# A two-layer bottleneck on one core: the first loads and the attention inputs change queues

## The chip, the core and the metric

The kernel runs on one core of a Trainium2 chip. A core has five engines with instruction streams of their own: TensorE (PE) for matrix products, VectorE (DVE) and ScalarE (ACT) for elementwise work, GpSimd (POOL) and SyncE (SP). They share an on-chip memory of 128 partitions (SBUF), the accumulators that PE writes (PSUM), and sixteen DMA engines that move data between SBUF and the main memory. A DMA is issued by an instruction in the stream of SP, ACT or POOL, and an instruction waits its turn in its stream: nothing behind a waiting instruction of an engine can start.

The metric is the device time of one execution in microseconds (us). The kernel before takes 2476.17 us, the median of 9 runs that lie between 2469.25 and 2484.35.

## The reference, cut to what matters

Sixteen images of 1024 channels and 32x32 pixels go through two bottleneck layers, all in float32. The first has a self-attention over a 3x3 neighbourhood in its middle, the second a 3x3 convolution.

```python
# layer 0
h = relu(bn(conv1x1(x, w_conv1)))                    # 1024 -> 256 channels
q, k = relu(bn(conv1x1(h, wq))), relu(bn(conv1x1(h, wk)))
v = bn(conv1x1(h, wv))
attn = softmax(sum over the 8 channels of a head of q * (unfold3x3(k) + pos_h + pos_w))
h = relu(bn(sum over the 9 places of unfold3x3(v) * attn))
x = relu(bn(conv1x1(h, w_conv3)) + x)                # 256 -> 1024
# layer 1
out = relu(bn(conv1x1(x, w1)))                       # 1024 -> 256
out = relu(bn(conv3x3(out, w2)))
x = relu(bn(conv1x1(out, w3)) + x)                   # 256 -> 1024
```

## The kernel before, in words

An image's 1024 channels are eight chunks of 128 channels (one per partition) by 1024 pixels, 512 KB each. The work of an image falls into stages on PE, and one list (`stages`) fixes their order for all sixteen images:

- conv1 (C): the eight chunks `x` times the weights `w1`, summed in PSUM (`reduce_part`, L346). ACT turns the sum into `h` (L975).
- qk (Q): from `h` the keys (`bnk`), the queries (`q`) and the position terms (`pos`); v (V): the values (`bnv`). The products are at L432 and L470.
- fused (F): the attended tensor `a` times `w3` plus the residual `s` (L377), and at once the first sum of layer 1 (L346).
- wino (W): the 3x3 convolution of four images together in Winograd form, `V` times `U` (L723).
- u3 (U): the last product plus the residual `r` (L377).

The stages run C, Q, V for images 0 to 3, then F of finished images between the C, Q, V of later ones. "C8 Q8 W0 V8" is a stretch of the list: image 8's queries are made directly before the Winograd stage of images 0 to 3, which is directly before image 8's values. Images 11 and 14 stand so before the stages of images 4 to 7 and 8 to 11.

The attention itself is DVE's work and runs beside PE's stages. It needs its inputs in another layout: one row per group of heads and quarter of the image. So `q`, `bnk`, `bnv` and `pos` are written to main memory and read back ("relay"). The writes: SP issues `bnk` and `bnv` (L456) and `q` (L490, two DMAs per image), ACT issues `pos` (L484, two per image). All reads back are issued by POOL (`relay`, L520). The position terms take a step that matters here: ACT writes them over the first half of `q` (`by_offset`, L479), so this instruction waits until the first `q` DMA has read that half.

POOL issues nearly all bulk transfers: the later images' chunks, the residuals and the Winograd forms (L322), and the results (L397). At a time eight tiles are there for loaded chunks (`credits`); a load is issued when the tile is free.

What happens before the first product is written by hand in `at_first`. ACT issues the first image's chunks, and between them the loads of the nine taps of the 3x3 weights (`load_taps`, two times three DMAs of 384 KB, L248), and then the last weights of both layers (`load_scaled`, four of 512 KB, L211). SP issues the first weights `w1` in eight pieces of 128 KB, one per chunk (L126), then `wqk` and `wv` (L128). `scale_rows` then turns a scale of 1024 channels, which lies over partitions, into one row in main memory (L221, `row`, 1024 elements of 4 bytes), and reads that row back into all partitions (L223, `scales`), once for each layer. From the taps ACT and DVE make the Winograd weights (`winograd_weights`, L259 to L269, in turns), which go to main memory (L281, `uw`, twelve DMAs of 768 KB); DVE then scales the last weights (L231).

In the built program each DMA of SP and ACT has one of eight semaphores, given out in turn over both engines, and each DMA of POOL one of eight others. A DMA waits until the one that had its semaphore before has landed. So a DMA of ACT can wait for one of SP.

Of the kernel before, what the change touches and what calls it, by code (L numbers as in the profile page):

```python
# [13 lines left out]
P = 128  # L14
# [4 lines left out]
NW = WID // P  # L19
# [6 lines left out]
CHUNKS = 8  # L26
NJ = 4
# [4 lines left out]
NPOS = 4  # L32
G = P // HEAD_DIM
# [38 lines left out]
def sa_bottleneck_kernel(ctx: ExitStack, tc: tile.TileContext, x, w1t, wqkvt, w3t, u1t, u2t, u3t, params, out):  # L72
    nc = tc.nc
# [25 lines left out]
    def source(name, half):  # L99

        if name[0] == "U":
            return uw[int(name[1]), half]
        if name in ("w3", "u3"):
            return ws[name == "u3", half]
        if name[1] == "1":
            src = {"w1": w1t, "u1": u1t}[name].rearrange("(c p) n -> p c n", p=P)
            return src[:, half * NC // 2 : (half + 1) * NC // 2]
        at = {"wqk": slice(0, 2 * WID), "wv": slice(2 * WID, 3 * WID)}[name]
        return wqkvt.rearrange("(c p) n -> p c n", p=P)[:, :, at]

    def more_weights():

        if not queue:
            return
        key = name, of, half = queue.pop(0)
        t = wpool.tile([P, HW], F32, tag="w", name=f"{name}{half}_{of[0]}")
        src = source(name, half)
        n, k = src.shape[-1], 1
        for d in src.shape[1:-1]:
            k *= d  # L120
        view = t[:, : k * n].rearrange("p (c n) -> p c n", n=n)
        if len(src.shape) == 4:
            view = t.rearrange("p (m j o) -> p m j o", m=NW, j=2)
        if of[1] == 0 and name == "w1":
            for c in range(k):
                nc.sync.dma_start(view[:, c], src[:, c])  # L126
        else:
            nc.sync.dma_start(view, src)  # L128
        pieces[key] = view

    def done_with(key):

        if last_use[key] == now[0]:
            more_weights()
# [3 lines left out]
    def col(name, j, n=1):  # L138
        return par[:, _COL[name] + j : _COL[name] + j + n]
# [65 lines left out]
    def load_scaled():  # L205

        rooms = vh.rearrange("p r w -> p (r w)"), hpool.tile([P, 2 * HW], F32, tag="h", name="scaled")
        for which, src in enumerate((w3t, u3t)):
            for half in range(2):
                at = rooms[which][:, half * HW :][:, :HW].rearrange("p (n o) -> p n o", n=NW)  # L210
                nc.scalar.dma_start(at, src.rearrange("(n p) o -> p n o", p=P)[:, :, halves(half)])  # L211
                scaled[which, half] = at

    def clear_hidden():
# [26 lines left out]
    def load_taps(m):  # L241
        n = 3 * WID

        tag, shape = (("e", [P, KK, JPIX]), ("bnv", [P, HEAD_DIM, HALO]))[m]
        t = apool.tile(shape, F32, tag=tag, name="g").rearrange("p a b -> p (a b)")
        g = [t[:, i * n : (i + 1) * n] for i in range(3)]
        for i in range(3):
            nc.scalar.dma_start(g[i], u2t[m * P : (m + 1) * P, i * n : (i + 1) * n])  # L248
        taps.append(g)

    def winograd_weights():
# [41 lines left out]
    def inside(t, n):  # L293
        return t[:, n, 1 : 1 + H, 1 : 1 + W]

    def rows(ap):
        return ap.rearrange("p (r w) -> p r w", w=W)

    def halves(half):
        return slice(half * HALF, (half + 1) * HALF)  # L300


    loads, loaded, stored, credits, freed = [], {}, {}, [CHUNKS], []

    def more_loads():

        while credits[0] and loads:
            kind, b, c = loads[0]
            if kind == "V":
                if forms.get(b, 0) < NK:  # L310
                    return
                src = form_room(b)[c[0], c[1]].rearrange("p k j e -> p (k j e)")
            elif kind == "r":
                if (b, c) not in stored:
                    return
                src = stored[b, c]
            else:
                src = x[b, c * P : (c + 1) * P, :]
            t = xpool.tile([P, NK * 2 * PART], F32, tag="x", name=f"{kind}_{b}_{c}".translate(str.maketrans(" ,", "__", "()")))
            t = t if kind == "V" else t[:, :HW]  # L320

            (nc.scalar if kind == "x" and b == 0 else nc.gpsimd).dma_start(t, src)  # L322
            loaded[loads.pop(0)] = t
            credits[0] -= 1
# [12 lines left out]
    def piece(name, half):  # L337
        return name, owner[now[0], name, half], half
# [83 lines left out]
    def project(b):  # L422

        h = hidden.pop(b)

        def conv(which, n):
            ps = psum.tile([P, HW], F32, tag="ps", name="ps")
            name, at = ("wqk", which * WID) if which < 2 else ("wv", 0)
            key, at = piece(name, 0), at + n * P
            for half in range(2):  # L430
                for m in range(NW):
                    nc.tensor.matmul(  # L432
                        ps[:, halves(half)],
                        pieces[key][:, m, at : at + P],
                        h[:, m, halves(half)],
                        start=(m == 0),
                        stop=(m == NW - 1),
                    )
            if n == NW - 1 and which:
                done_with(key)  # L440
            return ps

        def norm(dst, src, name, n, func):
            nc.scalar.activation(  # L444
                dst, src, func,
                bias=col(f"L0_conv_{name}_b", n), scale=col(f"L0_conv_{name}_s", n),
            )

        def halo(name, which, func):

            room, backs[name] = by_quarter(name, b, HALO, HEAD_DIM)
            for n in range(NW):
                norm(inside(kp, n), rows(conv(which, n)), name, n, func)

                block = kp[:, n]
                nc.sync.dma_start(  # L456
                    room[n], AP(block.tensor, block.offset, [block.ap[0], [JROWS * PW, NJ], [1, HALO]])
                )
                yield CHUNK

        backs = relaid[b] = {}
        q = hpool.tile([P, NW, HW], F32, tag="h", name=f"q_{b}")
        room, backs["q"] = by_quarter("q", b, JPIX, HEAD_DIM)

        def positions():

            ps = psum.tile([P, HW], F32, tag="ps", name="ps")
            for half in range(2):
                for n in range(NW):
                    nc.tensor.matmul(  # L470
                        ps[n * G * NPOS : (n + 1) * G * NPOS, halves(half)],
                        pos[:, n].rearrange("p g t -> p (g t)"),
                        q[:, n, halves(half)],
                        start=True,
                        stop=True,
                    )

            by_offset = q[:, 0, :]
            nc.scalar.activation(by_offset, ps, AF.Identity)  # L479

            room, backs["pos"] = by_quarter("pos", b, JPIX, NPOS)
            by_offset = by_offset.rearrange("p (j w) -> p j w", j=NJ)
            for n in range(NW):
                nc.scalar.dma_start(room[n], by_offset[n * G * NPOS : (n + 1) * G * NPOS])  # L484

        k = halo("bnk", 1, RELU)
        yield next(k)
        for n in range(NW):
            norm(q[:, n, :], conv(0, n), "bnq", n, RELU)
            nc.sync.dma_start(room[n], q[:, n, :].rearrange("p (j w) -> p j w", j=NJ))  # L490
            yield CHUNK
        yield next(k)
        positions()
        side.add(b)
        written.add(("qk", b))
        relay("qk", b)
        yield 2.5
        for n, cost in enumerate(halo("bnv", 2, AF.Identity)):
            if n:
                written.add(("v", b))  # L500
                relay("v", b)
            yield cost
# [140 lines left out]
    def form_room(b):  # L643
        b -= b % NK
        if b not in form_rooms:
            form_rooms[b] = dram.tile([NI, 3, P, NK, 2, PART], F32, tag=f"v{b}", name="v")
        return form_rooms[b]
# [465 lines left out]
    made = []  # L1113

    def at_first():
        credits[0] = 4
        more_loads()
        load_taps(0)
        credits[0] = 3
        more_loads()  # L1120
        load_taps(1)
        credits[0] = CHUNKS - 7
        more_loads()
        load_scaled()
        for _ in range(4):
            more_weights()
        side.first(winograd_weights(), 24.0, 0.0)
        side.first(scale_weights(), 24.0, 0.0)
        scale_rows()
        hooks["conv1", 2, 0] = clear_hidden  # L1130
# [44 lines left out]
```

## Time and profile before

| | before |
|---|---|
| median of 9 runs | 2476.17 us |
| the profiled execution, its run | 2480.11 us |
| the profiled execution, its span | 2478.2 us |
| PE busy | 2398.6 us (97%) |
| DVE busy | 2076.6 us (84%) |
| ACT busy | 919.1 us (37%) |
| POOL busy | 411.0 us (17%) |
| DMA | 709.94 MB, 286 GB/s over the span |
| x<-in_x_dram issued by ACT | 8 DMAs, 10.3 us to landing |
| q<-q issued by SP | 32 DMAs, 6.4 us to landing |
| pos<-q issued by ACT | 32 DMAs, 7.0 us to landing |

The span is the time from the first to the last instruction of the profiled execution; its run has 1.9 us around it. PE is busy for nearly all of it: the 80 us in which it is not are what any change of loads can win. An idle time of another engine costs nothing unless PE waits for it. In the lines of the profile, "out<-in" names the tiles, "xcount" the number of merged instructions, and what stands in brackets is the idle time of the engine before the group and what ended it.

### The profile page before, as it was taken

What the parts mean: (1) busy time and instruction counts of PE and PEld (TensorE: products, weight loads), DVE (VectorE), ACT (ScalarE), POOL (GpSimd) and SP (SyncE); (2) the same over time, 40 slices, a digit from 0 to 9 for tenths busy, and PEclk for the clock granted to TensorE, in tenths of its full rate; (3) what the DMA queues carried; (4) which work ended last, traced back from release to release, by engine and by line L of the source; (5) the groups of instructions that cost most, each with busy time, mean ns of one, the idle gap of its engine ahead of it and who ended that gap; (6) DMA issues with size and microseconds to landing.
All of it is one profiled execution on the core that took longest, in us unless ns stands there. A gap on an engine that the chain in (4) does not pass through costs nothing.

```text
span 2478.2 us, 18390 instructions
## 1 busy us (share of the span) xinstructions
PE 2398.6 (97%) x6144; PEld 1155.3 (47%) x6144; DVE 2076.6 (84%) x1631; ACT 919.1 (37%) x873; POOL 411.0 (17%) x777
## 2 busy tenths in 40 slices
PE   5999999999999998999999999999999999998998
PEld 2444444444456443444457443444466444434843
DVE  2799998989989999898889999799989999964700
ACT  1423232233222574324212564324222453343275
POOL 1110101010111122111111122111111121112122
PEclk9999999999999999999999999999999999999999
DMA  9978787878888899788789899689788897789878
GB/s 271 350 258 262 261 283 246 266 241 260 288 305 258 315 310 340 256 299 299 243 260 312 305 311 347 237 297 317 259 298 300 277 357 250 281 298 312 302 253 272
DMA packets 328429, 709.94 MB, mean 286 GB/s; under 512 B 22672, under 2 KB 201872, under 8 KB 319632
## 3 DMA queue, kind: packets, MB, share of 16 engines
q0 software_dynamic: 110592, 441.24, 50.1%
q1 hardware_dynamic: 205792, 250.45, 31.6%
q10 hardware_dynamic: 11952, 17.09, 2.6%
q8 instruction: 49, 0.80, 0.1%
q14 instruction: 44, 0.36, 0.0%
HBM read 433.67 MB, written 275.03 MB: 286 GB/s over the span
## 4 chain that ended last, share of the span: by engine, by line
PE 82%; DMA 9%; DVE 3%; issue 3%; ACT 2%; POOL 1%; ACTq 0%; SPq 0%; POOLq 0%; DVEq 0%
PE ps L346 33%; PE ps L377 26%; PE ps L432 12%; PE ps L723 9%; DMA out_dram<-r 4%; DMA q<-q 1%; DVE acc L590 1%; PE ps L470 1%; DVE acc L603 1%; DMA U<-uw 1%; DMA row<-bn_inv 1%; DMA row<-par 1%; DMA s<-in_x_dram 1%; ACT h L975 1%; DMA a<-a 0%
## 5 line engine op out<-in xcount | busy, mean ns | idle before, releaser
L377 PE MATMUL ps<-a,w 128*128 128x512 f32 x1024 | 464.9, 599 | 10.3 <-ACT ps L370 5.8
L346 PE MATMUL ps<-x,w 128*128 128x512 f32 x1024 | 446.6, 596 | 23.5 <-DMA x<-in_x_dram 23.5
L346 PE MATMUL ps<-s,u 128*128 128x512 f32 x1024 | 458.0, 592 | 1.1 <-ACT s L396 1.1
L377 PE MATMUL ps<-y,u 128*128 128x512 f32 x1024 | 443.7, 594 | 10.1 <-ACT ps L370 10.1
L539 DVE TENSOR_TENSOR prod<-qc,bnk 128x2048 f32<-128x2048 f32 x144 | 324.1, 2287 | 8.2 <-DMA a<-acc 6.5
L590 DVE TENSOR_TENSOR acc<-e,bnv 128x2048 f32<-128x2048 f32 x144 | 327.5, 2283 | 3.6
L346 PEld LDWEIGHTS ps<-x,w 128*128 128x128 f32 x1024 | 195.7, 191 | 271.2 <-issue 252.2
L377 PEld LDWEIGHTS ps<-a,w 128*128 128x128 f32 x1024 | 195.7, 192 | 261.8 <-issue 242.4
L396 ACT ACTIVATE s<-ps,par 128x1024 f32<-128x1024 f32 x128 | 142.4, 1113 | 466.3 <-PE ps L377 377.9
L377 PEld LDWEIGHTS ps<-y,u 128*128 128x128 f32 x1024 | 194.8, 191 | 257.1 <-issue 237.9
L346 PEld LDWEIGHTS ps<-s,u 128*128 128x128 f32 x1024 | 194.4, 190 | 246.4 <-issue 237.5
L603 DVE TENSOR_TENSOR acc<-acc 128x2048 f32<-128x2048 f32 x128 | 293.4, 2292 | 4.4
L432 PE MATMUL ps<-h,wqk 128*128 128x512 f32 x512 | 228.2, 600 | 12.1 <-ACT h L975 12.1
L397 POOL DMA_DIRECT2D r<-s x128 | 68.3, 534 | 732.6 <-ACT s L396 716.0
L396 ACT ACTIVATE r<-ps,bn_sh 128x1024 f32<-128x1024 f32 x128 | 141.7, 1107 | 103.0 <-PE ps L377 102.4
L544 DVE TENSOR_TENSOR prod<-prod 128x2048 f32<-128x2048 f32 (+1 forms) x80 | 166.2, 2077 | 2.3
L432 PEld LDWEIGHTS ps<-h,wqk 128*128 128x128 f32 x512 | 97.0, 192 | 140.9 <-issue 111.6
L370 ACT ACTIVATE ps<-r 128x1024 f32<-128x1024 f32 x128 | 130.4, 1021 | 59.2 <-DMA r<-r 47.3
L975 ACT ACTIVATE h<-ps,par 128x1024 f32<-128x1024 f32 x32 | 38.4, 1203 | 286.7 <-PE ps L346 286.7
L370 ACT ACTIVATE ps<-s 128x1024 f32<-128x1024 f32 x128 | 131.1, 1024 | 21.0 <-DMA s<-in_x_dram 17.1
L444 ACT ACTIVATE kp<-ps,par 128x1024 f32<-128x1024 f32 x64 | 77.2, 1206 | 136.3 <-PE ps L432 122.5
L746 ACT ACTIVATE z<-ps 128x1024 f32<-128x1024 f32 x48 | 49.1, 1024 | 184.3 <-PE ps L723 127.6
(307 smaller groups left out, 2258.3 us busy)
## 6 DMA issues: line engine op xcount, KB each, us to landing
s<-in_x_dram POOLq DMA_DIRECT2D x128, 512.0 KB, 6.4
r<-s POOLq DMA_DIRECT2D x128, 512.0 KB, 5.0
r<-r POOLq DMA_DIRECT2D x128, 512.0 KB, 5.8
out_dram<-r POOLq DMA_DIRECT2D x128, 512.0 KB, 6.5
x<-in_x_dram POOLq DMA_DIRECT2D x120, 512.0 KB, 5.2
v<-v SPq DMA_DIRECT2D x96, 408.0 KB, 5.2
U<-uw SPq DMA_DIRECT2D x72, 512.0 KB, 7.2
bnk<-kp SPq DMA_DIRECT2D x32, 680.0 KB, 7.6
```

What stands on the lines that cost most here:

```text
L346: nc.tensor.matmul(ps[n][:, halves(half)], wt[:, c % (NC // 2), n * P : (n + 1) * P], src[:, halves(half)], start=(c == 0), stop=(c == NC ...
L370: nc.scalar.activation(ps, t, AF.Identity)
L377: nc.tensor.matmul(self.ahead[o][:, halves(half)], pieces[key][:, n, o % (NC // 2) * P :][:, :P], self.src[:, n, halves(half)], start=Fals ...
L396: nc.scalar.activation(to_, ps, RELU, bias=self.shift(o), scale=1.0)
L397: nc.gpsimd.dma_start(to, t)
L432: nc.tensor.matmul(ps[:, halves(half)], pieces[key][:, m, at : at + P], h[:, m, halves(half)], start=(m == 0), stop=(m == NW - 1),)
L444: nc.scalar.activation(dst, src, func, bias=col(f"L0_conv_{name}_b", n), scale=col(f"L0_conv_{name}_s", n),)
L539: nc.vector.tensor_tensor(by_row(t[:, two]), by_row(qc), kc[:, :, i : i + JROWS, j : j + W], ALU.mult)
L544: nc.vector.tensor_add(u[:, :, 0:4], u[:, :, 0:4], u[:, :, 4:8])
L590: nc.vector.tensor_tensor(by_row(dst), rows(e[:, k, :]).unsqueeze(1).to_broadcast([P, HEAD_DIM, JROWS, W]), vc[:, :, i : i + JROWS, j : j ...
L603: nc.vector.tensor_add(acc, acc, t)
L723: nc.tensor.matmul(acc[i][:, at, :, n, :], pieces[key][:, m, at, n * P : (n + 1) * P], v[:, at, :, m * (TILES + TR) :][:, :, :TILES], star ...
```

## The change

Three things are changed. The first weights `w1` come in three DMAs (chunk 0; chunks 1 to 3; the second half) where there were eight. All eight chunks of the first image are issued by ACT one behind the other; the taps and the last weights no longer stand between and behind them in ACT's stream, but are issued by POOL, ahead of the second image's chunks. And for all sixteen images the two `q` DMAs and the two `pos` DMAs are issued by POOL, no longer by SP and ACT. No arithmetic and no byte moved is added or taken away, and the order of the instructions on PE and DVE stays.

```diff
@@ more_weights
         if of[1] == 0 and name == "w1":
-            for c in range(k):
-                nc.sync.dma_start(view[:, c], src[:, c])
+            for part in (slice(0, 1), slice(1, k)) if half == 0 else (slice(0, k),):
+                nc.sync.dma_start(view[:, part], src[:, part])
         else:
             nc.sync.dma_start(view, src)
@@ load_scaled
-                nc.scalar.dma_start(at, src.rearrange("(n p) o -> p n o", p=P)[:, :, halves(half)])
+                nc.gpsimd.dma_start(at, src.rearrange("(n p) o -> p n o", p=P)[:, :, halves(half)])
@@ load_taps
-            nc.scalar.dma_start(g[i], u2t[m * P : (m + 1) * P, i * n : (i + 1) * n])
+            nc.gpsimd.dma_start(g[i], u2t[m * P : (m + 1) * P, i * n : (i + 1) * n])
@@ project, positions
             for n in range(NW):
-                nc.scalar.dma_start(room[n], by_offset[n * G * NPOS : (n + 1) * G * NPOS])
+                nc.gpsimd.dma_start(room[n], by_offset[n * G * NPOS : (n + 1) * G * NPOS])
@@ project
             norm(q[:, n, :], conv(0, n), "bnq", n, RELU)
-            nc.sync.dma_start(room[n], q[:, n, :].rearrange("p (j w) -> p j w", j=NJ))
+            nc.gpsimd.dma_start(room[n], q[:, n, :].rearrange("p (j w) -> p j w", j=NJ))
@@ at_first
-        credits[0] = 4
         more_loads()
-        load_taps(0)
-        credits[0] = 3
-        more_loads()
-        load_taps(1)
-        credits[0] = CHUNKS - 7
-        more_loads()
+        for m in range(NW):
+            load_taps(m)
         load_scaled()
```

## The prediction

> **What bounds the kernel now.** I read the page first: PE is busy for 2398.6 of 2478.2 us, so about 80 us can be won, and only where PE stands still. The sum of PE's waits names the largest: 23.5 us for `x<-in_x_dram`, four times, all at the start. PE's timeline of the first 80 us (start, length, engine, group, idle before it):
>
> ```profile
> 9.53 15.79 PE L346 MATMUL ps<-x,w 128*128 128x512 f32 x32 [9.53 <-DMA x<-in_x_dram]
> 33.25 5.56 PE L346 MATMUL ps<-x,w 128*128 128x512 f32 x8 [7.93 <-DMA x<-in_x_dram]
> 41.79 7.13 PE L346 MATMUL ps<-x,w 128*128 128x512 f32 x16 [2.97 <-DMA x<-in_x_dram]
> 51.99 3.70 PE L346 MATMUL ps<-x,w 128*128 128x512 f32 x8 [3.07 <-DMA x<-in_x_dram]
> 62.53 16.59 PE L432 MATMUL ps<-h,wqk 128*128 128x512 f32 x32 [6.84 <-ACT h L975]
> ```
>
> A chunk is 8 matmuls, 3.43 us at full clock. The first stage needs 27.5 us and ends at 55.7; then PE waits 6.84 us more for `h`. For every later image that wait is 0.44 us. The first 62.53 us hold 30.3 us of idle time; all later PE gaps together are some 38 us, in many pieces under 7 us.
>
> ACT's timeline says why `h` is late: ACT issues DMAs until 49, makes its part of the Winograd weights after that, and `h` stands behind three rounds of it:
>
> ```profile
> 46.87 0.33 ACTq L322 DMA_DIRECT2D x<-in_x_dram  x1
> ...
> 49.46 0.84 ACT L259 ACTIVATE g<-g 128x768 f32<-128x768 f32 x1 [45.67 <-DMA g<-in_u2t_dram]
> ...
> 61.29 2.28 ACT L975 ACTIVATE h<-ps,par 128x1024 f32<-128x1024 f32 x2
> ```
>
> Why are the chunks late? Not only because they were issued late. The table by stretches (last columns: TensorE clock, DMA share, GB/s) shows two stretches in which the DMA engines are busy and move next to nothing; the list of DMA issues (KB each, us to landing) shows who is in flight then:
>
> ```profile
> 6.00:12.00 6.00, 2.47 (x3) 1.18 (x4) 0.39 (x4) 0.00 (x0) 0.00 (x0) 1.00 0.99 353
> 15.00:21.00 6.00, 6.00 (x16) 2.65 (x15) 0.00 (x0) 0.00 (x0) 1.21 (x2) 1.00 0.72 54
> 27.00:33.00 6.00, 0.00 (x0) 0.00 (x0) 0.96 (x1) 0.00 (x0) 0.00 (x0) 0.77 1.06 388
> 33.00:40.00 7.00, 5.56 (x8) 2.22 (x8) 0.00 (x0) 0.00 (x0) 0.53 (x1) 0.71 1.12 82
> ...
> row<-par SPq DMA_DIRECT2D x1, 4.0 KB, 16.5
> row<-bn_inv SPq DMA_DIRECT2D x1, 4.0 KB, 16.6
> ```
>
> The two `row` writes of 1024 four-byte elements sit in exactly these stretches (issued 5.55, landed 22.05; issued 22.51, landed 39.09). The change leaves them.
>
> The second place is the start of the Winograd stage of images 0 to 3. Lines of the timelines of SP, POOL, ACT and PE:
>
> ```profile
> 701.87 3.79 SPq L490 DMA_DIRECT2D q<-q  x2
> ...
> 706.61 0.53 POOL L322 DMA_DIRECT2D V__2_2351<-v  x1 [10.59 <-DMA v<-v]
> ...
> 708.16 0.53 POOL L322 DMA_DIRECT2D V__0_2357<-v  x1
> ...
> 712.07 1.02 ACT L479 ACTIVATE q<-ps 128x1024 f32<-128x1024 f32 x1 [3.35 <-DMA q<-q]
> ...
> 728.02 6.34 PE L723 MATMUL ps<-V__2_2351,U 128*128 128x256 f32 x16 [4.55 <-DMA U<-uw]
> ```
>
> ACT's L479 waits for the first `q` DMA, and the copies `z` (L746), for which PE waits, stand behind it. POOL is blocked until 706.61 at that place.
>
> **What the Trainium skill says.** "DMA: Bandwidth & Descriptors", section "Issuing engines are not separate DMA queues": transfers of SP, ACT and POOL run on the same 16 DMA engines and interleave, so another queue saves only issue time. The trace agrees: from 27 to 33 us three queues together moved 388 GB/s, from 6 to 12 us two moved 353. The same page, "Queues, rings and completion order": each DMA engine takes one queue's descriptors in order and goes round between the queues. The trace fits: eight `V` loads issued from 693.78 to 708.16 landed in that order, at 7.0 to 14.8 us each. Its "Specifications" call transfers under 512 B read-modify-write; here two 4 KB transfers in 4-byte pieces took 16.5 us each.
>
> **The change part by part.** All times are of the profiled execution (span 2478.2).
>
> *First weights, 8 DMAs to 3.* Issue is 0.43 us each, 2.2 us saved on SP. The bytes stay, and `x` chunk 0 landed at 9.49 with the first piece long there (3.16): worth 0.
>
> *First loads.* In the built program ACT's chunks 0 and 1 now wait for nothing, 2 and 3 for pieces of `w1`, 4 and 5 for chunks 0 and 1, 6 for the first `row`, 7 for chunk 2. POOL puts six taps and two weights (3.4 MB) in at once from about 4 us, two more when the first taps have landed. So three queues share from 5 us where there were two. I take equal shares by bytes.
> - SP must pass 1.84 MB (`w1`, `wqk`, `wv`) before `row`. At 5 us some 0.7 are through (0 to 6 us moved 0.9 MB in all); 1.14 MB at a third of 370 GB/s take 9.3 us. The first slow stretch begins at 14 where it began at 12; ACT and POOL have 1.15 MB each.
> - It lasts 10 us (12 to 22) and carried about 1.1 MB (247 GB/s for 3 us, 54 for 6). At 24.5 ACT has 1.75 of its 4.19 MB: chunks 0 to 2. Chunks 6 and 7 are issued here.
> - The second slow stretch came 11 us after the first `row` landed, so at 35.5. Until then 11 us at 388 GB/s are 4.2 MB; `scales` takes 0.5 of it, ACT and POOL 1.85 each. ACT is at 3.6 MB: through chunk 5, most of 6.
> - Seven us at 82 GB/s give ACT 0.3 MB. At 42.5, 0.3 MB of chunk 7 are left: 2 us at a third to a half of 378 GB/s, about 1 us to land: 45.3.
> - Chunk 7's products take 3.7 us (line at 51.99) to 5.6 (line at 33.25, low clock); I take 4.3. First stage ends at 49.6 instead of 55.7.
> - ACT is free at about 25 and the first taps are there, so the three rounds (12 us, 49.5 to 61.3) end by 38 and hide in the loading; the wait for `h` is 0.44. The queries start at 50.0 instead of 62.53: **12.5 us gained.** If that cover were gone, 6.4 of them would be lost.
>
> Does the gain last? Other PE waits move with it. DVE's first logits begin after its Winograd and scaling work (to 107 us), but from 81 on that work follows ACT's L479 of image 0 and so PE; it moves by the same 12.5.
>
> *`q` and `pos` to POOL, 64 DMAs.* A POOL issue is 0.53 us for 128 rows. The trace shows none there with 512 pieces of 1 KB; between 0.53 and four times that, 2.1. In ten images POOL stands idle for 26 to 28 us around the place, with its last load landed, so even 2.1 us plus 3 to land meets L479's natural time, 7.6 us after the first `q`: cost 0. ACT is rid of 1.3 us of issue per image; only image 6 shows PE gaps behind it (0.94 and 0.35 at 503 and 508): 1.3 gained. Image 12: 0.4 gained.
> The Winograd stages differ, as the built order shows where `q` stands in POOL's stream.
> - Image 8: behind all eight `V` loads. Issue at 708.7 instead of 701.87, data behind 2.2 MB of which the last landed at 723.0. With `q` (1 MB) gone from SP's queue those may land 1 to 2 us earlier. `q` lands at 723 to 724.5, where L479 had it at 712. `z` then lets PE go on at 725 to 727 instead of 716.3. PE would have stood still from 723.5 to 728.0 anyway (`U`, now earlier too). Following the six groups of 3.45 us, and 2.7 us of low clock that the old gap also had: 4 to 5.5 later; I take **5 lost.** ACT's saved `pos` issue (2 us) is in it.
> - Image 11: the first `q` stands before the `V` loads: L479 no longer waits 8.89 us, and PE's gap of 3.17 before L723 (and 1.7 of low clock) goes. But the second `q` and `pos` (1 MB) now stand before `V__1_4420`, which landed at 1300 for a use at 1304: some 5 us later, it is late next. Between 4 gained and 3 lost: 0.
> - Image 14: behind eight `V` loads, the last landed at 1834.5; L479 ran at 1835.0. 1 us later, 1.3 of `pos` issue saved: 0, at worst 3 lost.
>
> Reads back behind a waiting `q` or `pos` (image 6: `qc` 9 us later) have 20 us and more of attention work in DVE before use: 0.
>
> Sum: -12.5 - 1.3 - 0.4 + 5 = **-9.2 us**: span 2469.0. The profiled run (2480.1) lies 3.9 above the median of the runs; taken from that median, 2467.
>
> **Rivals.** *B, the last chunk gets in before the second `row`:* it lacks 0.6 MB at 35.5. If POOL starts later or gets a smaller share, chunk 7 lands at 36, queries start at 41: 21.5 gained in front, 18 in all: 2458. For it: POOL's queue was the slowest to start. Against: from 27 to 33 us its share was as large as ACT's.
> *C, the taps crowd the chunks:* 4.5 MB more in flight early; the first `row` lands at 27, chunk 7 at 50, queries at 54.5: 8 - 3.3 = 4.7 gained: 2471.5.
> *D, slower: POOL's order blocks ACT.* In the three Winograd stages `q` or a `V` waits in POOL's queue, and L479 holds ACT's `z`. Image 8 costs 11 (no overlap with the `U` wait), image 11 5, image 14 3, less 1.7: 17 lost, with a front at 10 to 12: 2482. It decides once `q` of image 8 lands after 728 and `V__1_4420` after 1307. For it: POOL waited 10.6 and 11.9 us for `v` there. Against: SP's queue is relieved by as much.
> *E, the change does not do what it says:* excluded, the order of instructions shows all of it.
>
> **Chances.** A (forecast, 2461 to 2473 by itself) 0.48, B 0.20, C 0.17, D 0.15. About 0.2%, 5 us, is what can be told from no change. Faster: 0.41 of A, B, 0.04 of C, 0.65; same 0.07 of A, 0.12 of C, 0.03 of D, 0.22; slower: 0.01 of C, 0.12 of D, 0.13. The range leaves out the ends of B and D: 2453 to 2480.
>
> **What would show it.** Right: `L432` starts at 48 to 52 with a wait of 0.4; the two slow stretches are still there, near 14 to 24 and 35 to 42; chunk 7 lands after the second; L479 of image 8 waits 12 us or more; the 8.89 us wait of image 11 is gone. Wrong: chunk 7 before 38 (B); PE waits for `x` of the second image; L479 waits in images that had none; DVE idles before `qc`.

## The result and the profile after

The kernel after the change takes 2466.20 us (median of 17 runs, 2456.12 to 2473.67), the kernel before beside it 2476.12 us (54 runs). The ratio is 0.9958, with a 95% interval from 0.9947 to 0.9968: 9.9 us faster, where 2467 was forecast. Run again later beside the kernel before, the change gave 0.9962 (0.9950 to 0.9973).

The two profiled executions differ by more than the medians: 22.1 us of span. The one of before lies 4 us above its median, the one of after 8 us below. So only part of what lies between the two traces belongs to the change, and a difference of 2 or 3 us at one place of them is not proof.

PE's timeline of the first 80 us of the kernel after:

```profile
16.25 22.24 PE L346 MATMUL ps<-x,w 128*128 128x512 f32 x48 [16.25 <-DMA x<-in_x_dram]
40.12 7.42 PE L346 MATMUL ps<-x,w 128*128 128x512 f32 x16 [1.63 <-DMA x<-in_x_dram]
47.38 1.02 PE L432 MATMUL ps<-h,wqk 128*128 128x512 f32 x2
48.83 13.14 PE L432 MATMUL ps<-h,wqk 128*128 128x512 f32 x30 [0.44 <-ACT h L975]
62.83 1.07 PE L470 MATMUL ps<-q,pos 128*64 128x512 f32 x2 [0.85 <-ACT q L444]
65.56 1.93 PE L470 MATMUL ps<-q,pos 128*64 128x512 f32 x6 [1.65 <-ACT q L444]
```

The queries start 15.2 us earlier (47.38 for 62.53), and the wait for `h` is the 0.44 us that twelve other images show too. But the path to this is not the one forecast. PE starts on chunk 0 at 16.25, not at 9.5, and six chunks are used without a pause. At the end of the list stands something new: PE waits twice for ACT's `q`. ACT's timeline and the list of DMA issues of the first 60 us:

```profile
3.57 29.57 ACTq L322 DMA_DIRECT2D x<-in_x_dram  x8
33.19 0.84 ACT L259 ACTIVATE g<-g 128x768 f32<-128x768 f32 x1 [29.41 <-DMA row<-par]
...
45.86 1.20 ACT L975 ACTIVATE h<-ps,par 128x1024 f32<-128x1024 f32 x1 [0.75 <-PE ps L346]
```
```profile
row<-par SPq DMA_DIRECT2D x1, 4.0 KB, 28.9
row<-bn_inv SPq DMA_DIRECT2D x1, 4.0 KB, 15.2
```

ACT issues the eight chunks until 33: the last two wait for the first `row`, whose 4 KB now take 28.9 us to land where they took 16.5. The table by stretches (last columns: clock, DMA share, GB/s) shows where the two slow stretches are now:

```profile
9.00:14.00 5.00, 0.00 (x0) 0.00 (x0) 0.00 (x0) 0.00 (x0) 0.00 (x0) 1.00 1.13 145
15.00:27.00 12.00, 10.75 (x22) 4.86 (x23) 0.96 (x1) 0.00 (x0) 2.51 (x4) 1.00 1.02 402
...
42.00:47.00 5.00, 4.98 (x13) 1.95 (x11) 4.55 (x12) 3.05 (x7) 0.53 (x1) 1.00 0.65 60
```

The first holds chunk 0 back and is over by 15, though `row` lands only at 32; the second comes when the chunks are nearly through (the last lands at 43.8). After chunk 0 PE waits no more than 1.63 us: the start of the stage sets its end.

The slow stretch is not all that holds chunk 0 back. ACT issues it at 3.57 us, but in the first 8 us nearly all that moves is SP's. The list of DMA queues for these 8 us (q1 is SP's, q10 ACT's, q0 POOL's; packets, MB, share of the engines' time):

```profile
q1 hardware_dynamic: 1860, 1.79, 71.8%
q10 hardware_dynamic: 161, 0.12, 5.7%
q0 software_dynamic: 8, 0.05, 1.5%
```

So SP's weights (1.84 MB) are nearly through before the other two queues have begun, and the row's small pieces, which stand behind the weights, come early.

At the Winograd stage of images 0 to 3, by the timelines of POOL, ACT and PE:

```profile
686.71 0.53 POOL L322 DMA_DIRECT2D V__2_2346<-v  x1 [8.64 <-DMA v<-v]
...
688.78 0.77 POOL L490 DMA_DIRECT2D q<-q  x1
...
703.16 1.02 ACT L479 ACTIVATE q<-ps 128x1024 f32<-128x1024 f32 x1 [9.87 <-DMA q<-q]
...
705.15 5.39 PE L723 MATMUL ps<-V__1_2342,U 128*128 128x256 f32 x16 [4.14 <-ACT z L746]
710.38 3.62 PE L723 MATMUL ps<-V__1_2344,U 128*128 128x256 f32 x16
713.83 3.62 PE L723 MATMUL ps<-V__2_2346,U 128*128 128x256 f32 x16
```

L479 waits 9.87 us behind `q` (3.35 before), and PE pays 4.14 for it. But `V__2`, which waited 4.55 us for `U` before and then ran its group in 6.34 us instead of 3.62, now goes on without a pause. From the start of image 8's queries to the sixth group it was 41.3 us before and is 39.8 us after (PE's timelines, two lines of before and two of after):

```profile
692.86 1.02 PE L432 MATMUL ps<-h,wqk 128*128 128x512 f32 x2
734.20 3.62 PE L723 MATMUL ps<-V__2_2353,U 128*128 128x256 f32 x16
...
677.44 1.02 PE L432 MATMUL ps<-h,wqk 128*128 128x512 f32 x2
717.28 3.62 PE L723 MATMUL ps<-V__2_2348,U 128*128 128x256 f32 x16
```

The place gained 1.5 us in these two traces.

### The profile page after: what moved, and what is told of

It reads as the page before. It is cut to its first block, busy times and chain, and to the rows that moved or that the text cites. A ratio compares the mean times of both kernels' runs of the same rounds, so it can differ in the third digit from the quotient of the medians.

```text
span 2456.1 us, 18395 instructions
## 1 busy us (share of the span) xinstructions
PE 2390.4 (97%) x6144; PEld 1152.9 (47%) x6144; DVE 2076.6 (85%) x1631; ACT 918.7 (37%) x873; POOL 463.1 (19%) x851
## 3 DMA queue, kind: packets, MB, share of 16 engines
q0 software_dynamic: 118816, 470.86, 54.5%
## 4 chain that ended last, share of the span: by engine, by line
PE 79%; DMA 13%; DVE 3%; issue 3%; ACT 1%; POOL 1%; SPq 0%; POOLq 0%; ACTq 0%; DVEq 0%
PE ps L346 34%; PE ps L377 23%; PE ps L432 12%; PE ps L723 10%; DMA out_dram<-r 8%; DMA row<-par 1%; PE ps L470 1%; DMA bnk<-kp 1%; DVE acc L590 1%; DVE acc L603 1%; DMA s<-in_x_dram 1%; DMA row<-bn_inv 1%; ACT h L975 1%; POOL r L322 1%; DMA uw<-u 1%
## 5 line engine op out<-in xcount | busy, mean ns | idle before, releaser
L346 PE MATMUL ps<-x,w 128*128 128x512 f32 x1024 | 444.1, 594 | 17.9 <-DMA x<-in_x_dram 17.9
L346 PE MATMUL ps<-s,u 128*128 128x512 f32 x1024 | 458.2, 592 | 1.7 <-ACT s L396 1.7
L346 PEld LDWEIGHTS ps<-x,w 128*128 128x128 f32 x1024 | 194.9, 191 | 263.8 <-issue 260.0
L346 PEld LDWEIGHTS ps<-s,u 128*128 128x128 f32 x1024 | 194.3, 190 | 247.4 <-issue 238.0
L432 PE MATMUL ps<-h,wqk 128*128 128x512 f32 x512 | 225.8, 595 | 5.7 <-ACT h L975 5.7
L432 PEld LDWEIGHTS ps<-h,wqk 128*128 128x128 f32 x512 | 96.2, 190 | 132.7 <-issue 110.0
L370 ACT ACTIVATE ps<-r 128x1024 f32<-128x1024 f32 x128 | 130.4, 1021 | 56.0 <-DMA r<-r 48.4
L370 ACT ACTIVATE ps<-s 128x1024 f32<-128x1024 f32 x128 | 131.1, 1025 | 20.3 <-DMA s<-in_x_dram 17.9
L322 POOL DMA_DIRECT2D r<-r x128 | 68.2, 533 | 295.0 <-DMA out_dram<-r 182.3
```

What stands on the lines that cost most here:

```text
L346: nc.tensor.matmul(ps[n][:, halves(half)], wt[:, c % (NC // 2), n * P : (n + 1) * P], src[:, halves(half)], start=(c == 0), stop=(c == NC ...
L370: nc.scalar.activation(ps, t, AF.Identity)
L432: nc.tensor.matmul(ps[:, halves(half)], pieces[key][:, m, at : at + P], h[:, m, halves(half)], start=(m == 0), stop=(m == NW - 1),)
```

## The experiments

Each kernel was timed beside the kernel before on the same chip, so ratios compare across the list, absolute times don't (the kernel before had medians of 2477.1, 2467.1, 2469.9 and 2468.6 us on the four chips). "At the queries" is the start of L432 for image 0: 62.53 before, 47.38 in the change. Some of the expectations count from the product behind the wait for `h` (48.8 in the change), and put the end of the first stage at 48.4, where it is 47.5.

### The front alone, and q with positions alone

The first kernel is the change with L490 back on SP and L484 back on ACT; the second is the kernel before with only these two lines moved.

```diff
-            nc.gpsimd.dma_start(room[n], q[:, n, :].rearrange("p (j w) -> p j w", j=NJ))
+            nc.sync.dma_start(room[n], q[:, n, :].rearrange("p (j w) -> p j w", j=NJ))
```

> Only the first loads are changed; q goes back to SP and pos to ACT. If the gain is the front's (my theory: 12.5 us forecast, about 13.5 read from the trace), the ratio to before is 0.9945 to 0.9960, the same as the whole change, and the first query products start at 47 to 50 us. If q and pos on POOL bring half (rival: the profiled execution of the change is 22 us shorter, the front only 13.5 of it), the ratio is 0.9975 or more. L479 of image 11 waits 8 to 9 us again.

> Only q and pos go to POOL; the first loads are as before. My forecast gave this part a loss of 3.3 us (ratio 1.0013): 5 lost at image 8, 1.7 gained elsewhere. The trace of the change suggests that image 8 costs nothing: then 0 to 3 us are gained (0.9988 to 1.0000). Rival: it brings half of the gain, 5 us or more (0.998 or less).

Front alone: 0.9960 (0.9943 to 0.9976). `q` and positions alone: 1.0039 (1.0026 to 1.0053), so 10 us slower. The front alone gives the whole gain, as the first expectation had it; the second kernel is slower than any of its expectations. The product of the two ratios would be 0.9999; the change measured 0.9958. So the parts don't add up: beside the new front, `q` and positions cost nothing that the times can show. (In the first kernel L479 of image 11 waits 8.03 us again, as expected.)

PE's and SP's timelines of the front-only kernel:

```profile
48.09 14.24 PE L432 MATMUL ps<-h,wqk 128*128 128x512 f32 x32 [0.50 <-ACT h L975]
65.85 1.07 PE L470 MATMUL ps<-q,pos 128*64 128x512 f32 x2 [3.52 <-ACT q L444]
...
50.73 0.33 SPq L223 DMA_DIRECT2D scales<-row  x1
51.17 12.21 SPq L281 DMA_DIRECT2D uw<-u  x4
...
66.10 1.21 SPq L490 DMA_DIRECT2D q<-q  x1
```

The 3.52 us look like the price of `q` on SP. The order of times excludes that: PE waits until 65.85, and SP issues the first `q` at 66.10. What holds ACT's `q` are ACT's Winograd rounds, which wait for their tiles until `uw` is written; and SP writes no `uw` before the second `row` has landed (50.73). By the traces, image 0 loses more the later that row lands. From the start of the queries to the first chunk of image 1 it takes 23.4 us in the kernels below that have no such row. Here it is 8.6 us more, with the row landing 2.6 us after the start of the queries; in the change's two traces it is 3.6 and 3.2 us more (row 0.5 and 0.8 after), with `q` and positions by POOL in image 0 alone 2.3 (0.2 before), and with the first weights in eight pieces 0.4 (3.3 before).

In the second kernel the trace shows two losses at PE, by the timelines of PE and ACT (the last line is from before):

```profile
873.27 27.15 PE L377 MATMUL ps<-y,u 128*128 128x512 f32 x56 [3.30 <-ACT ps L370]
...
1306.34 5.89 PE L723 MATMUL ps<-V__1_4420,U 128*128 128x256 f32 x13 [2.95 <-issue]
...
871.10 1.21 ACT L444 ACTIVATE kp<-ps,par 128x1024 f32<-128x1024 f32 x1 [9.27 <-DMA bnk<-kp]
...
866.84 1.21 ACT L444 ACTIVATE kp<-ps,par 128x1024 f32<-128x1024 f32 x1 [3.66 <-DMA bnk<-kp]
```

The second is the one forecast: `V__1_4420` late behind `q` and `pos` (it lands at 1306.25). With the low clock after it, it loses 6.6 us, after 5.3 gained just before. The first was not thought of: ACT fills `kp` with the values only when the `bnk` write has read it, and that write, still on SP, now runs beside `q` and `pos` of another queue, which is probably why it takes longer (15.6 us to landing, 10.4 before). ACT waits 9.27 us for it, 3.66 before; the copy that fills PSUM ahead of PE's sum (L370) and PE stand behind, and PE falls back by 6.4 us. Over the whole execution ACT waited for `bnk` 13.7 us before, 28.5 here, and 26.7 and 21.8 in the change's two traces. There PE lost 1.1 and 3.2 us against before at this place, so the price is in the change too, only smaller.

### The end of the span

At the last product this second kernel was 4.6 us late, at the end of the span 10.5. The rest lies after the last DMA issue of POOL (timeline), up to the end of the span (page):

```profile
2478.07 0.53 POOL L397 DMA_DIRECT2D out_dram<-r  x1 [2.39 <-ACT r L396]
```
```profile
span 2488.7 us, 18399 instructions
```

That is 10.6 us; 4.8 before (2473.44 to 2478.2). To test whether it goes by the number of POOL's issues, the four last weights were put on POOL as well:

```diff
-                nc.scalar.dma_start(at, src.rearrange("(n p) o -> p n o", p=P)[:, :, halves(half)])
+                nc.gpsimd.dma_start(at, src.rearrange("(n p) o -> p n o", p=P)[:, :, halves(half)])
```

> The kernel before with q, positions and, in addition, the four last weights by GpSimd's queue (836 DMA issues of GpSimd; the run with q and positions alone had 832, and a last stretch of 10.1 us after its last issue, where the kernel before with 768 and the change with 842 have 4.2 and 4.3). Theory that the count of GpSimd's issues sets the closing stretch, and not what they carry: it falls back to 4 to 5 us, the rest of the trace is as with q and positions alone, and the median is near 2481.5 us (2487.7 less 6), ratio 1.0015 to 1.0025. Rival, that q and positions themselves lengthen the end: the stretch stays near 10 us and the median near 2487.5, ratio 1.004. If moving four weights matters by itself, the first image's queries start elsewhere than at 62 to 64 us.

The same two lines of this kernel:

```profile
2479.49 0.53 POOL L397 DMA_DIRECT2D out_dram<-r  x1 [0.34 <-ACT r L396]
```
```profile
span 2484.2 us, 18401 instructions
```

Down to 4.7 us. Over all traces:

| DMA issues of POOL | kernels | last issue to end, us |
|---|---|---|
| 768 | before | 4.8 |
| 778 | front alone | 5.3 |
| 782 | three below | 5.8, 5.7, 5.8 |
| 832 | `q`, positions alone; taps last on ACT | 10.6, 10.6 |
| 836 | this one | 4.7 |
| 842 | the change (twice) and four others | 4.7 to 4.9 |

So in the traces it goes by the count and not by what is carried, and repeats to 0.2 us. Why, stays open. The medians do not show the gain: this kernel gave 1.0040 (1.0025 to 1.0056), the same as without the four weights, where 1.0015 to 1.0025 was expected. A later start does not explain it: the queries of image 0 start 2.2 us later than before, but those of image 1 at 115.21, where it is 115.36 before and 115.44 in the kernel with `q` and positions alone. With intervals this wide, a gain of some us and none are both possible.

### q and positions by POOL in image 0 alone; the change once more

```diff
-            nc.gpsimd.dma_start(room[n], q[:, n, :].rearrange("p (j w) -> p j w", j=NJ))
+            (nc.gpsimd if b == 0 else nc.sync).dma_start(room[n], q[:, n, :].rearrange("p (j w) -> p j w", j=NJ))
```

> The change, but q and positions go by GpSimd's queue in image 0 alone; in images 1 to 15 they are back on SyncE's and ScalarE's. Theory: of q and positions only image 0 gains by the move (5.6 us at its attention product, where SyncE's queue is full of Winograd transforms), and images 8 and 11 lose by it, so this gives the front-only version's 2467.8 less 5.6, about 2462 us, ratio 0.994, below the change's 2466.2. Rival: the move pays, or costs nothing, in the later images too: then 2466 us or more, ratio 0.9955 to 0.997, no better than the change.

> The change once more, as it is: a second trace, to see which differences from the trace of before come again. Expected: first stage ends at 48.4 within 1 us, image 0's attention without the wait of 3.5 us, the closing stretch 4.3 us; median 2466 us. The parts of the difference that no step of the change explains (about 5 us between the 1427th and the 1534th us) come again if they belong to the change, and do not if they are chance of one execution: then the span is near 2464 instead of 2456.1.

The first gave 0.9957 (0.9942 to 0.9972), the change beside it 0.9962 (0.9950 to 0.9973), the front alone above 0.9960: three choices for these 64 DMAs that can't be told apart. The theory of 5.6 us at image 0 is not borne out, for the reason found above: by the order of times, that loss hangs on the second row's landing and not on the queue of `q`. The change's second trace has a span of 2455.9 us, the queries at 45.27, and the same steps as its first to 3 us; but of 3.4 us that the first gained between 1427 and 1534 us, which no step explains, only 1.3 came again. Both are compared with a single trace of before, and the second comes from a chip where the kernel before has another median (2467.1 for 2476.1); what those us are stays open.

### Rows later, and taps last on ACT

The change with `scale_rows` called after the first image's last chunk, and the change with taps and last weights on ACT behind all chunks:

```diff
-        scale_rows()
+        hooks["conv1", 0, NC - 1] = scale_rows
```
```diff
-            nc.gpsimd.dma_start(g[i], u2t[m * P : (m + 1) * P, i * n : (i + 1) * n])
+            nc.scalar.dma_start(g[i], u2t[m * P : (m + 1) * P, i * n : (i + 1) * n])
```

> The change, with scale_rows issued after the first image's last chunk instead of at the start. If the row writes hold chunks 6 and 7 (a semaphore wait on the first row, and the slow stretch), all chunks land by 32 us, the first stage ends at 44 to 45 instead of 48.4, the queries start 3 to 4 us earlier and the time falls by as much: ratio to before 0.9940 to 0.9948. Rival: the slow stretches only move to the loads of the second image and the Winograd weights, and the time stays at 0.9958 or gets worse.

> The change, with taps and last weights issued by ACT behind all first chunks instead of by POOL. If POOL's early taps slow the chunks (rival C of the prediction), chunk 0 lands at 9 to 10 us instead of 16 and the first stage ends 2 to 5 us earlier. If the cover of the Winograd rounds is what counts (my theory: ACT must be free of DMA issue early), ACT issues until 40 us or later, h waits 4 to 8 us behind the rounds, and the queries start at 50 to 55: 3 to 6 us slower than the change, ratio to before 0.997 to 0.998.

Rows later: 0.9979 (0.9969 to 0.9990), so the rival was right. PE's timeline: the queries start at 41.69, 20.8 us ahead of before, and 15.8 of it are lost by the third image, half of them at once, where image 1 waits for `h`:

```profile
41.69 1.02 PE L432 MATMUL ps<-h,wqk 128*128 128x512 f32 x2
...
106.09 16.67 PE L432 MATMUL ps<-h,wqk 128*128 128x512 f32 x32 [7.94 <-ACT h L975]
```

So the rows do hold up the first stage (chunk 0 lands at 12.3 here and the last chunk at 32.8; 16.1 and 43.8 in the change); moved, they land at 59 and 72, and what is lost is lost there.

Taps last on ACT: 1.0045 (1.0025 to 1.0066), worse than expected, with 832 issues and the long end. ACT's and PE's timelines:

```profile
30.07 18.69 ACTq L248 DMA_DIRECT2D g<-in_u2t_dram  x6
...
62.90 2.28 ACT L975 ACTIVATE h<-ps,par 128x1024 f32<-128x1024 f32 x2
...
64.14 16.11 PE L432 MATMUL ps<-h,wqk 128*128 128x512 f32 x31 [23.71 <-ACT h L975]
```

The first stage ends at 40.4 (7 us ahead of the change's first trace, 5 of its second; chunk 0 lands at 10.7), yet `h` waits 23.71 us behind ACT's issues and rounds. So taps on POOL cost the chunks something; what they win is ACT's stream.

### First weights in eight pieces again

```diff
-            for part in (slice(0, 1), slice(1, k)) if half == 0 else (slice(0, k),):
-                nc.sync.dma_start(view[:, part], src[:, part])
+            for c in range(k):
+                nc.sync.dma_start(view[:, c], src[:, c])
```

> The change, but the first weights of image 0 go in eight pieces of 128 KB again instead of three. Theory: the number of pieces is worth nothing, since the first stage ends with the last chunk of the input (43.8 us) and not with a weight: queries between 48 and 50 us, ratio 0.9955 to 0.997 as for the change. Rival: five more issues of 0.46 us on SyncE hold row<-par back by 2 to 3 us (issued at 3.35 us in the change) and with it the last two chunks: queries 2 to 3 us later, and the same at the end, ratio 0.9965 to 0.998.

SP's and PE's timelines:

```profile
6.07 0.92 SPq L221 DMA_DIRECT2D row<-par  x1
37.07 0.34 SPq L223 DMA_DIRECT2D scales<-row  x1
...
42.61 6.77 PE L346 MATMUL ps<-x,w 128*128 128x512 f32 x8 [5.26 <-DMA x<-in_x_dram]
...
53.41 1.02 PE L432 MATMUL ps<-h,wqk 128*128 128x512 f32 x2
```

The rival was right, by more than its size: `row` is issued 2.7 us later (6.07 for 3.35), lands 5 us later, PE waits for a chunk in the middle of the stage, and the queries start 6 us later than in the change's first trace (8 than in its second). Later issue is not all: in eight pieces the weights also move slower. By 9 us SP's queue has moved 0.95 MB here, and all of its 1.84 MB in the change. Part of the loss comes back: the second row lands before the queries, ACT's `q` is not held, and at the second image's queries 2.8 (5.3) us are left. The ratio, 0.9968 (0.9959 to 0.9976), is 2 us worse than the change's and overlaps with it; so the loss is shown at the front and only likely at the end.

### Rows by TensorE

If the 4-byte rows are the limit, the remedy is not to write them. A matrix of ones times the scales on a diagonal gives the same row in all partitions (cut: `ones` and `eye` are made ahead of it on POOL, the diagonal on VectorE):

```diff
-            row = dram.tile([NC, P], F32, tag=f"row{which}", name="row")
-            nc.sync.dma_start(row.rearrange("o p -> p o"), scale)
+            nc.vector.tensor_tensor(
+                diag, eye.unsqueeze(1).to_broadcast([P, NC, P]), scale.unsqueeze(2).to_broadcast([P, NC, P]), ALU.mult)
+            ps = psum.tile([P, HW], F32, tag="ps", name="ps")
+            for half in range(2):
+                nc.tensor.matmul(ps[:, halves(half)], ones, room[:, which * HW :][:, halves(half)], start=True, stop=True)
             t = zpool.tile([P, HW], F32, tag="z", name="scales")
-            nc.sync.dma_start(t, AP(row.tensor, row.offset, [[0, P], [1, C]]))
+            nc.vector.tensor_copy(t, ps)
```

Four kernels: the products ahead of image 0 with `eye` made late; the same with `eye` made first on POOL; in addition taps and last weights only after chunk 0 is used, `q` and positions by POOL in image 0 alone; and last, the products behind chunk 0. The added lines shift the numbers: L366 or L370 is L346 above, L452 or L456 is L432, L490 is L470; the products for the rows are L239 or L243.

> The change, but the two rows of scales are spread over the partitions by TensorE (a product of a matrix of ones with the scales on a diagonal) instead of through DRAM in 4-byte pieces: row<-par and row<-bn_inv are gone, four matmuls and two VectorE copies take their place. Theory: the 4-byte pieces slow every transfer beside them and hold up the issue of the last two chunks until 32.3 us; without them the last chunk lands near 35 to 38 us, the queries start at 39 to 42 us (change: 48.8), and the 7 to 9 us stay to the end: 2457 to 2460 us, ratio 0.992 to 0.993. Rival (what happened when the rows were only moved later): the second image's loads or the Winograd weights take it back, 2464 to 2468 us. Second rival: the rows cost nothing, the bytes set the time of the last chunk: queries at 46 to 49 us.

> The change with the two rows of scales spread by TensorE as in the run before, but with the diagonal made before anything else on GpSimd, so that the four products run while TensorE waits for chunk 0; there they stood ahead of image 0 and let it begin at 25.7 us, though all eight chunks had landed by 29. Theory: without 4-byte pieces the chunks no longer set the first stage; it begins with chunk 0 at about 16 us (the taps still share its transfer) and then runs through in 27.4 us of products: end near 43.5, queries near 44.5 us (change: 48.8 and 46.4 in its two traces), 2 to 4 us gained over the change at the end, ratio 0.994 to 0.9955. Rival: the loss returns in image 1 or in the Winograd weights: ratio 0.9955 to 0.997.

> The run with early rows by TensorE, and taps and last weights are issued by GpSimd only after TensorE has used chunk 0, and q and positions go by GpSimd in image 0 alone. Theory: the taps are what moved chunk 0 from 9.5 to 16.1 us in the change; without them beside it chunk 0 lands at 8 to 10 us, the first stage is TensorE's 27.4 us of products plus small waits, queries at 38 to 41 us; Winograd's ScalarE work on the taps starts near 25 us instead of 13. About 8 us gained over the change at the front and 2 to 3 from q and positions: ratio 0.9915 to 0.9935. Rival: h then waits on ScalarE behind Winograd's work, which waits for the taps (as the 23.7 us when the taps were put last on ScalarE), and the front is worth no more than the change's: ratio 0.995 to 0.997.

> The run before, but the four products that spread the rows stand behind chunk 0 of image 0 in TensorE's order instead of ahead of it; taps and last weights again follow chunk 0, q and positions go by GpSimd in image 0 alone. There all chunks had landed by 19.5 us, chunk 0 by 10.6, and TensorE began with chunk 0 only at 17.3 because the products for the rows stood ahead. Theory: now TensorE alone sets the first stage: it starts at 10.6 us, runs 27.4 us of products for image 0, 3.5 for the rows and loses 2 to 4 at a low clock at its start: queries at 42.5 to 44.5 us (45.7 there), 1 to 3 us gained to the end, ratio 0.9915 to 0.993. Rival: VectorE's copies of the rows, or the later taps, hold Winograd's transforms and with them ScalarE's h or the second image: queries at 46 us or later, ratio 0.993 to 0.995.

| | queries | ratio to before, interval |
|---|---|---|
| the change | 47.4, 45.3 | 0.9958 (0.9947 to 0.9968) |
| rows by TensorE, late | 54.3 | 0.9968 (0.9951 to 0.9985) |
| rows by TensorE, early | 45.8 | 0.9926 (0.9906 to 0.9945) |
| and taps after chunk 0 | 45.7 | 0.9927 (0.9910 to 0.9944) |
| and rows after chunk 0 | 43.7 | 0.9915 (0.9896 to 0.9935) |

In the first, my own products were the bound: they waited for the diagonal until 17.1, and image 0 stood behind them until 25.7, with nearly all chunks there. With them early (stretches, then PE's timeline, of the second kernel):

```profile
9.00:14.00 5.00, 3.35 (x4) 0.74 (x3) 1.61 (x2) 0.94 (x2) 1.54 (x3) 1.00 1.02 413
27.00:32.00 5.00, 5.00 (x13) 2.18 (x12) 4.48 (x12) 2.39 (x7) 0.53 (x1) 1.00 1.01 399
```
```profile
17.09 28.85 PE L366 MATMUL ps<-x,w 128*128 128x512 f32 x64
...
60.31 1.94 PE L490 MATMUL ps<-q,pos 128*64 128x512 f32 x8
```

From 9 to 14 us the engines move 413 GB/s where the change moved 145; chunk 0 lands at 11.6, the last at 31.0. PE begins with chunk 0 only at 17.09, here too behind the rows' products, then never waits, and the queries start about when they do in the change. What is gained at the front comes after them: the wait for ACT's `q` is gone, since no row stands ahead of `uw` in SP's stream (its first `uw` goes out at 26.9 us, at 48.4 in the change). At the second image's queries the kernel is 5.2 and 2.7 us ahead of the change's two traces. That was not in the expectation. By the ratios the gain over the change is 8 us, where 2 to 4 were expected; against the same two traces another 2.7 and 4.8 us lie between 1424 and 1527 us (in the time of before), where no step explains them. How much of the gain is the end of the slow stretches, and how much the freed `uw`, these kernels don't separate. Without the taps beside them (third kernel) chunk 0 lands at 10.6 and the last at 19.5; but PE starts at 17.28, again behind the rows' products, the queries start at 45.7 and not at 38 to 41, and nothing is gained.

Over all runs with the first weights in three pieces, chunk 0 lands at 10.5 to 10.7 without taps beside it (with a row in one of the three), at 11.6 to 13.1 with taps and no row, and at 13.2 to 16.9 with both, in the four traces that have the change's own front. In these four the stretch from 9 to 14 us moved 367, 191, 145 and 170 GB/s, in the order of chunk 0 at 13.2, 14.4, 16.1 and 16.9. So by these single traces the taps alone cost chunk 0 some 1 to 2.5 us, and the slow stretch, which is not there in every execution, up to 4 more.

In the fourth, PE's timeline has chunk 0 on arrival and no wait until `h`:

```profile
10.61 5.74 PE L370 MATMUL ps<-x,w 128*128 128x512 f32 x8 [10.61 <-DMA x<-in_x_dram]
16.19 3.60 PE L243 MATMUL ps<-diag 128*128 128x512 f32 x8
19.62 24.20 PE L370 MATMUL ps<-x,w 128*128 128x512 f32 x56
43.66 1.02 PE L456 MATMUL ps<-h,wqk 128*128 128x512 f32 x2
```

The queries start where expected (43.7, for 42.5 to 44.5). At 0.9915 it is faster than before and than the change, whose interval lies wholly above it; so are the two kernels above it in the table. Among the last three the intervals overlap.

## Why the prediction was right

The time and the direction came out (-9.2 forecast, -9.9 measured), and so did the place: the front alone gives it. That the total fits to within 1 us is in good part luck. Inside the front, a late start and the waits that it spared cancelled. Outside it, the steps at images 6, 8, 11 and 14 came out better in the trace than forecast: with 13.5 at the front (up to the second image) and 1.1 lost behind `bnk` they sum to some 18 us of gain, and the two traces differ by 22.1, where the medians differ by 9.9. That trace of before lies 4 us above its median and that of after 8 below; what evens it out in the other executions, the record does not show.

- *First weights, "worth 0".* Off. The step looked at when the pieces land, not at what stands behind them in SP's stream. Eight pieces issue `row` 2.7 us later, and the queries start 6 us later; 2.8 of these are left at the second image.
- *First loads, "12.5 us gained".* Right in sum (15.2 in the trace), wrong in its terms. The step that failed is the equal shares of three queues from 5 us on: in the first 8 us SP's queue moved 1.79 MB, ACT's 0.12 and POOL's 0.05. That chunk 0 would stay at its 9.49 was taken for granted with it, and failed: 16.1, behind SP's weights, beside the taps and through the slow stretch. The first slow stretch was put at 14 to 24 by counting SP's bytes at a third of the rate; they were through sooner, and the stretch lay at 9 to 14. `row` lands at 32.3 and not 24.5: its last pieces are still under way while full queues move 402 GB/s; chunks 6 and 7 go out 8 us later than computed. And the second stretch came at 42 to 47, not at 35.5 ahead of the last chunk. Forecast were a start at 9.5 and some 12 us of waits after it; it was a start at 16.25 and 1.63 us.
- *The wait for `h`, 0.44.* Right (the line holds for twelve of the fifteen later images, not for each), and the cover named for it was the right one: with ACT held back, the wait became 23.71 us.
- *What is late next at the front.* Missed. Behind the second `row`, `uw` and with it ACT's `q` are late: image 0 loses 3.6 us in the change and 8.6 in the front-only kernel, where it lost 2.0 to the low clock before, so of the 15.2 us 13.5 are left.
- *Image 8, "5 lost".* The mechanism was right (L479 waits 9.87 us, `z` holds PE 4.14), the size not: `q` was issued 11.3 us after the queries' start, not 15.8, as POOL's wait for `v` ended earlier against PE. It landed before 703.2, 25.7 us after that start, where 723 to 724.5 less 692.86, over 30, were computed. With the `U` wait gone, 1.5 us were gained where 5 lost were forecast.
- *Image 11, "0" and image 14, "0".* The exchange happened as described: the gap before the third group went, and `V__1` was late by 1.56 us in its place. The trace nets 1.9 and 0.3 us of gain. *Image 6* gained 1.9 for 1.3. *`q` issue on POOL*, bounded by 0.53 and 2.1 us, is 0.77 us, hidden.
- *"Cost 0" in the other images.* Not safe: alone, the move made ACT wait for `bnk` and PE 3.30 us behind it, and in the change 1.1 to 3.2 us are lost there. Why it costs 10 us alone and nothing beside the new front is only in part explained (the long end at 832 issues is a candidate for 5.8 of them).
- *Rivals.* B came half true: the last chunk did get in ahead of most of the second slow stretch, but 8 us later than B had it. C's crowding is real: the first `row` landed at 32.3, later even than C's 27, and without taps on POOL it landed at 21.9, the last chunk at 34.1, and the stage ended 7 us earlier. C's 54.5 us were not reached, as the last chunk came at 43.8 and not at 50. D's waits are there, but smaller: PE waits 4.14 us where D has a loss of 11, and 1.56 where it has 5.

The Trainium skill names what is wrong with the rows. "DMA: Bandwidth & Descriptors", section "Rules for kernel authors", says that a transfer with a strided last dimension becomes one descriptor per element, and advises to make the last dimension contiguous. The traces agree: the first 60 us have 2799 packets under 512 bytes in the change and 752 with the rows by TensorE early, 2047 fewer, and the two rows have 2048 elements. This case adds what it does to others: 145 and 60 GB/s for all queues together in the two stretches, and 413 from 9 to 14 us without the rows. "TensorE: Matmul & The Clock Gate", section "What's actually happening", says that the array runs at half clock after an idle spell until it has been busy for about 3.4 us. The traces agree: the first eight products of the last kernel took 5.74 us where the next eight of the same shape took 3.60, and the group behind the 4.14 us wait at image 8 took 5.39 where its neighbours take 3.62. That is 2.1 and 1.8 us more; half clock for 3.4 us would cost 1.7, an estimate from the page's figure.

## What to carry to other kernels

When a loading stage is slow, look for stretches where the DMA engines are busy and move little, and at what tiny transfer is in flight; take that transfer away before reordering the large ones, since moved, it cost more elsewhere here (0.9979, for 0.9958 unmoved). An instruction that looks free can decide when the one behind it is issued: follow each queue past the DMA that you change. After a gain at the front ask what then stands behind the same old bound; here it was ACT's `q` behind `uw` behind a 4 KB row. And a forecast that meets the total may still have its terms wrong: check it term by term.

## What was not expected of the hardware

- The time from POOL's last DMA issue to the end of the span goes, in these traces, by the number of its issues: 4.8 us at 768, 5.3 at 778, 5.8 at 782, 10.6 at 832, 4.7 at 836 and 842.
- A write of 4 KB in 4-byte pieces took 12.6 to 31 us; only part of that time slowed the others down (5 us of 28.9 in the change's first trace), and in one trace of the same front the first slow stretch is absent (367 GB/s from 9 to 14 us).
- Three queues with work at once did not share alike: in the first 8 us of the change SP's moved 1.79 MB, ACT's 0.12 and POOL's 0.05.
- The issue of a `q` DMA in 1 KB pieces took POOL 0.77 us, of one with whole rows 0.53.
